# Making all pixel planes of the split maps on ScalarE and GpSimd, with second buffers for them

## The chip, the cores and the metric

The kernel runs on one core of a Trainium2 chip. The core has five engines, each with its own queue that is worked off in order: TensorE (PE in the profile, with PEld for its weight loads), VectorE (DVE), ScalarE (ACT), GpSimd (POOL) and SyncE (SP, which here only issues transfers). They wait for each other by semaphores. The metric is the time of the whole program on the device, in microseconds (us). Three runs of the kernel before took 6669.03, 6680.48 and 6695.74 us, so the median is 6680.48.

## The reference, cut to what matters

The program computes two blocks, one after the other, on four images of 96 channels and 128x128 pixels.

The first block is a state-space layer: projection, depthwise convolution, four directional scans, a layer norm and a projection back to 96 channels. The change does not touch it.

The second block normalises each image and splits it at zero into two maps x1 and x2 (positive and negative part, each with a scale and a shift of its own). From them come three 3x3 convolutions over 96 channels, and a fourth whose weights are made from two of the results:

```python
x, x1, x2 = relu_split_norm(groupnorm(x), ...)
key   = unfold(conv3x3(x1, aw1));  qry = unfold(conv3x3(x2, aw2))
attn  = softmax(key @ qry.T / sqrt(C * 9))            # one set of C x C x 3 x 3 weights per image
out   = conv3x3(conv3x3(x1, aw3), attn)               # and conv3x3(x2, w_conv2) besides
```

A last step normalises the two results, mixes them with a 1x1 convolution and adds the residual.

## The kernel before, in words

**Planes.** For images 1 to 3 the 3x3 convolutions are done with fewer products: along a row, every four output pixels are made from six products, and each product needs one "plane", a fixed combination of neighbouring input pixels. So each map (x1, x2 and the value map v) is kept in DRAM as six planes (`x1p`, `x2p`, `vp`). For input pixels p(k), the six planes are sums and differences of p(k+2) - 4 p(k), of p(k+2) - p(k) and of the latter doubled. `planes_of` (L1354) makes them, for eight rows of 128 pixels and 96 channels at a time (for v: six rows on 128 partitions). It has two ways to do so:

- `at_once` (L1374) does all on VectorE, with nine instructions: L1379, L1380 and L1384 make differences into the tile `diff`, L1386 (two instructions) and L1372 (four) make the planes in the tile `plv`. Every one of them reads both inputs from SBUF.
- `scaled` (L1390) makes two scaled copies on ScalarE, `x4` (L1393, the input times four) and `x2` (L1394, half of it times two). Then `differences` (L1397) makes the planes with ten GpSimd instructions: L1402 to L1407, and four at L1372, into the tile `pl`. L1372 is a helper's line, shared by both ways.

`store_planes` (L1441) sends the finished tile to DRAM from SyncE's queue (L1443).

**The split.** `split_norm` (L1063) goes over an image in 16 tiles of eight rows. For each tile it makes x1 and x2 (L1225 on ScalarE into PSUM, L1229 on VectorE into a tile `half`), and then the planes of each. The argument `vector` chooses the way: in the kernel before, the planes of x1 go by `scaled` and those of x2 by `at_once`. The `half` tiles are two for x1 and one for x2. The scaled copies `x4` have two buffers; `x2`, `pl`, `plv` and `diff` have one.

**The attention.** `attention` (L1925) works on strips of 12 rows. A first pass over 11 strips makes key, query and value (matmuls at L1470 and L1485). ScalarE copies results out of PSUM (L1541), VectorE combines them (L1555 to L1563) into a ring of two strips and into the tile `own`. GpSimd copies 32 channels of each strip from the ring to `own` (L1974, three instructions, twice per strip), and the planes of the value map are made from `own` by `scaled` in two calls per strip (with single buffers). ScalarE also copies shifted inputs (L1904), and transposed pieces for the attention weights (L1751). Then the attention weights are made, and a second pass over 11 strips does the last convolution. Image 0 is done without planes of x1 and x2 (`direct_maps`, with the planes of its value map made by `lift`, L2122, on VectorE); its second pass is the same as that of the others.

**The order of the work.** Each part is a generator that emits instructions and yields a cost. `co_run` (L290) interleaves the attention of image b with a "light" chain: the norm and split of image b+1, and then the closing step of image b-1. `Later` (L305) puts off follow-up steps by some ticks. From the emitted program a scheduler fixes the order of each engine's queue before anything runs. Three splits lie in the program: that of image 1 beside the end of image 0's first pass and its second pass, that of image 2 beside the attention of image 1, and that of image 3 beside the attention of image 2. Image 3's attention runs with no split beside it.

Of the kernel before, what the change touches and what calls it, by code (L numbers as in the profile page):

```python
# [9 lines left out]
F32 = mybir.dt.float32  # L10
# [7 lines left out]
C = 96  # L18
# [15 lines left out]
PB = TN + 1  # L34
PP = PB * TW
# [18 lines left out]
RS = SN // W  # L54
# [14 lines left out]
def kernel(  # L69
# [101 lines left out]
    def col(name, width=1, bufs=None):  # L171
        return small.tile([C, width], F32, name=name, tag=name, bufs=bufs)
# [108 lines left out]
    def part(ps, *shape):  # L281
        n = 1
        for d in shape[1:]:
            n *= d
        t = bank(ps)[: shape[0], :n]
        return t if len(shape) == 2 else t.rearrange("p (a b) -> p a b", b=shape[2])
# [3 lines left out]
    def co_run(left, right, pace):  # L290


        owed = 0.0
        for cost in left:
            owed += cost * pace
            while owed > 0:
                got = next(right, 0)
                if got == 0:
                    return
                if got is None:  # L300
                    owed = 0.0
                    break
                owed -= got
# [39 lines left out]
    def chain(*gens):  # L343
        for g in gens:
            yield from g

    def drain(gen):
        for _ in gen:
            pass
# [713 lines left out]
    def split_norm(xnew, x1d, x2d, stats, keep, cnt, ps, side, planes, vector, done):  # L1063


        with ExitStack() as pools:
# [37 lines left out]
            p2 = p1.enter_context(tc.tile_pool(name="n1", bufs=2, side=side))  # L1104
            for i in range(NS):
                y = ahead.pop(0)
                piece(i + 3)
                r = p2.tile([C, SN], F32, name="xr")
# [12 lines left out]
            p2 = pools.enter_context(tc.tile_pool(name="n2", bufs=2, side=side))  # L1121
# [45 lines left out]
            rs, rh, half = col("rs", 2), col("rh", 2), col("half", 2)  # L1167
# [19 lines left out]
            def stored(i, m, h):  # L1187
# [7 lines left out]
                return lambda: nc.scalar.dma_start(m[:, at : at + RS * PW], h)  # L1195

            half = [
                [p2.tile([C, RS * PP], F32, name=f"half{j}{k}", bufs=1) for k in range(2 - j)]
                for j in range(2)
                if planes  # L1200
            ]
# [2 lines left out]
            for i in range(NS):  # L1204
                y = ahead.pop(0)
                piece(i + 3)
                for side_, m in ((0, x1d), (1, x2d)):
                    op = ALU.is_le if side_ else ALU.is_gt
                    if planes:
                        h = half[side_][i % len(half[side_])]  # L1210
                        v, to = (
                            t.rearrange("p (a b) -> p a b", b=b)[:, :, 0:TN]
                            for t, b in ((y, TN), (h, PB))
                        )
                        k, parts = TW * R, 2
                    else:
# [3 lines left out]
                        v, to = y.rearrange("p (h w) -> p h w", w=W), hv[:, :, 1:PW]  # L1220
                        k, parts = RS, 1
                    for a in range(0, k * parts, k):
                        x, o = v[:, a : a + k], to[:, a : a + k]
                        f = part(ps, C, k, TN) if planes else o
# [24 lines left out]
    def new_planes(name):  # L1249

        m = dram.tile([C, NP, H + 3, TN], F32, name=name, tag=name, bufs=1)
        for h in (0, H + 1, H + 2):
            nc.sync.dma_start(m[:, :, h], zeros[:, 0:TN].unsqueeze(1).to_broadcast([C, NP, TN]))
        return m
# [99 lines left out]
    def planes_of(later, pool, t, r, then, most=RS, vector=False, bufs=2, p=C):  # L1354

        a2 = AA * AA
        v = t[:, : r * PP].rearrange("p (h x) -> p h x", x=PP)

        def planes(name, bufs):
            pl = pool.tile([p, NP, most * TN], F32, name=name, bufs=bufs)[:, :, : r * TN]
            return pl, [pl[:, i].rearrange("p (h t) -> p h t", t=TN) for i in range(NP)]

        def sums(eng, mid, outer, to):
            f1, f2 = mid[:, :, 0:TN], mid[:, :, PB : PB + TN]
            f3, f0 = outer[:, :, 0:TN], outer[:, :, TN:]
            for i, op, x, y in (
                (1, eng.tensor_add, f2, f1), (2, eng.tensor_sub, f2, f1),
                (0, eng.tensor_sub, f2, f0), (5, eng.tensor_sub, f3, f1),  # L1370
            ):
                op(to[i], x, y)  # L1372

        def at_once():  # L1374
            f = pool.tile([p, most, 6 * TN + 4], F32, name="diff", bufs=1)[:, :r]
            mid, outer, df = f[:, :, : 2 * PB], f[:, :, 2 * PB : 130], f[:, :, 130:]
            pl, to = planes("plv", 1)
            stt = nc.vector.scalar_tensor_tensor
            stt(mid, v[:, :, : 2 * PB], -a2, v[:, :, 2 * PB :], ALU.mult, ALU.add)  # L1379
            stt(  # L1380
                outer, v[:, :, 2 * PB : 2 * PB + 2 * TN], -a2, v[:, :, 1 : 1 + 2 * TN],
                ALU.mult, ALU.add,
            )
            nc.vector.tensor_sub(df, v[:, :, 2 * PB :], v[:, :, : 2 * PB])  # L1384
            for i, f in ((3, AA), (4, -AA)):
                stt(to[i], df[:, :, 0:TN], f, df[:, :, PB : PB + TN], ALU.mult, ALU.add)  # L1386
            sums(nc.vector, mid, outer, to)
            later(lambda: then(pl))

        def scaled():  # L1390
            x4 = pool.tile([p, most * PP], F32, name="x4", bufs=bufs)[:, : r * PP]
            x2 = pool.tile([p, most, 2, PB], F32, name="x2", bufs=1)[:, :r]
            nc.scalar.mul(x4, t[:, : r * PP], a2)  # L1393
            nc.scalar.mul(x2, v.rearrange("p h (k b) -> p h k b", b=PB)[:, :, 0:TW:2], AA)  # L1394
            later(lambda: differences(x4.rearrange("p (h x) -> p h x", x=PP), x2))

        def differences(x4, x2):  # L1397
            mid, outer = x4[:, :, : 2 * PB], x4[:, :, 2 * PB : 2 * PB + 2 * TN]
            d1 = x2[:, :, 0, 0:TN]
            pl, to = planes("pl", 1)  # L1400
            sub, add = nc.gpsimd.tensor_sub, nc.gpsimd.tensor_add
            sub(mid, v[:, :, 2 * PB :], mid)  # L1402
            sub(outer, v[:, :, 1 : 1 + 2 * TN], outer)
            sub(to[4], v[:, :, 3 * PB : 3 * PB + TN], v[:, :, PB : PB + TN])
            sub(d1, x2[:, :, 1, 0:TN], d1)
            add(to[3], to[4], d1)
            sub(to[4], to[4], d1)  # L1407
            sums(nc.gpsimd, mid, outer, to)
            later(lambda: then(pl), 2)

        return at_once if vector else scaled
# [829 lines left out]
    class Image:  # L2241
# [27 lines left out]
        def split(self, ps, side, vector=lambda i, second: False):  # L2269
            halves = (self.x1p, self.x2p) if self.b else (self.x1d, self.x2d)  # L2270
            yield from split_norm(
                self.xnew, *halves, self.stats, self.keep, self.cnt, ps, side, self.b > 0, vector,
                self.done,
            )
# [40 lines left out]
    with tc.tile_pool(name="wp", bufs=1, side="left") as wp:  # L2315
# [7 lines left out]
        for images, pace in (([0], 0.25), ([1], 0.75), ([2, 3], 1.35)):  # L2323
            left = projections(images, weights, stats, wp, psl)
            if images[0] == 0:
# [4 lines left out]
                while ready[0] < 2:  # L2330
                    next(left)
                maps = [new_map(n) for n in ("x1d", "x2d", "vd")]
                planes = [
                    [new_planes(f"{n}{i}") for n in ("x1p", "x2p", "vp")] for i in range(2)
                ]
# [9 lines left out]
    imgs = {0: Image(0)}  # L2345
# [9 lines left out]
    psr = ctx.enter_context(tc.tile_pool(name="psr", bufs=2, space=PSUM, side="right"))  # L2355
# [1 line left out]
    imgs[0].lifting = True  # L2357
    light = chain(
        imgs[1].norm(yms[0][1], psr, "right"),
        imgs[1].split(psr, "right", lambda i, second: second),  # L2360
    )
    co_run(left, light, 1.0)
    drain(left)
# [20 lines left out]
    for b in range(NB):  # L2384
        after = []
        if b:
            if b > 1:
                drain(light)
            imgs[b].begin()
            if b + 1 < NB:  # L2390
                imgs[b + 1] = Image(b + 1)
                after.append(imgs[b + 1].norm(yms[(b + 1) // 2][(b + 1) % 2], psr, "right"))
                after.append(imgs[b + 1].split(psr, "right", lambda i, second: second))
            after.append(imgs[b - 1].close(psr, "right"))
        light = chain(light, *after)
        left = imgs[b].attend(at)
        co_run(left, light, 1.0 if b else 1.5)
        drain(left)
# [77 lines left out]
```

## Time and profile before

| | us |
|---|---|
| median of three runs | 6680.48 (6669.03 to 6695.74) |
| the profiled execution | 6664.87 |
| its span in the profile | 6663.1 |
| TensorE busy | 5393.7 |
| VectorE busy | 4885.0 |
| ScalarE busy | 3810.5 |
| GpSimd busy | 3437.4 |

The splits of images 1, 2 and 3 make their planes from 3636 to 4010 us, from 4392 to 4738 us and from 5273 to 5599 us of this span. In each of them VectorE and GpSimd both make 16 sets of planes.

A row for a group of instructions reads: line, engine, operation, output<-input tiles, shapes, x count | busy us, mean ns of one | idle time of the engine just before them, and what ended it. A row for a stretch of time gives the busy us of each engine with the number of its instructions. A row of waits gives who waited for whom, the us in total, how often, and the longest.

### The profile page before, as it was taken

The page shows a single profiled execution, that of the slowest core. Times are in us where ns is not written, and L with a number is a line of the kernel's source. Part 1 is how long each engine was busy: PE and PEld are TensorE (multiplying, and loading weights), DVE is VectorE, ACT ScalarE, POOL GpSimd, SP SyncE. Part 2 cuts the span into 40 slices and gives each one's busy share as a digit, 9 for nine tenths or more (in the row PEclk, how much of TensorE's full clock was granted, in tenths as well). Part 3 has the DMA queues.
Part 4 walks back from the last instruction along what each step waited for, and adds up shares of the span by engine and source line. Part 5 has one row for each costly group of instructions (what it writes and reads, how often), then busy time and mean ns, then how long its engine had stood idle before and what let it go on. Part 6 is the DMA issues. An engine that isn't in the chain of part 4 may idle for free. (4 is left out here: it accounts for less than half of the span.)

```text
span 6663.1 us, 76540 instructions
## 1 busy us (share of the span) xinstructions
PE 5393.7 (81%) x23256; PEld 2343.1 (35%) x23256; DVE 4885.0 (73%) x7737; ACT 3810.5 (57%) x4751; POOL 3437.4 (52%) x2683
## 2 busy tenths in 40 slices
PE   5889978988887626989985579877889777878996
PEld 2333323322221103434433243444333454335642
DVE  3247778988997568979756884588865788887557
ACT  1257768777776576767534554565444664535552
POOL 2236658878786436969622363465124574023410
PEclk9999989988997758999997788988879887989987
DMA  7766777866765666765676766556765555865454
GB/s 166 173 156 180 198 212 199 225 180 171 221 186 162 186 175 208 203 194 175 196 189 175 205 167 165 157 148 163 200 182 159 145 159 153 227 164 145 103 149 143
DMA packets 882102, 1176.27 MB, mean 177 GB/s; under 512 B 215230, under 2 KB 740102, under 8 KB 869212
## 3 DMA queue, kind: packets, MB, share of 16 engines
q1 hardware_dynamic: 858076, 1116.43, 61.9%
q0 software_dynamic: 16208, 38.42, 2.1%
q10 hardware_dynamic: 7408, 16.53, 0.8%
q8 instruction: 187, 3.06, 0.2%
q14 instruction: 223, 1.83, 0.1%
HBM read 766.61 MB, written 334.57 MB: 165 GB/s over the span
## 5 line engine op out<-in xcount | busy, mean ns | idle before, releaser
L621 PE MATMUL bank<-y,wp 128*128 128x512 f32 (+3 forms) x3584 | 1315.3, 623 | 84.3 <-DMA y<-y 34.0
L854 POOL TENSOR_TENSOR y<-y,dl 128x1024 f32<-128x1024 f32 x384 | 1051.3, 2738 | 267.8 <-DVE dl L846 237.1
L821 POOL TENSOR_TENSOR dl<-dl,u 128x1024 f32<-128x1024 f32 x384 | 1007.5, 2624 | 228.0 <-ACT dA L797 116.3
L842 DVE TENSOR_TENSOR_SCAN dA<-dA,pBC 128x512 f32<-128x512 f32 x768 | 981.7, 1278 | 30.7
L1470 PE MATMUL two<-ya,wd 128*64 128x192 f32 (+3 forms) x2376 | 590.5, 426 | 189.5 <-ACT odd L1541 106.6
L735 PE MATMUL pBC<-xr,wbc 60*128 60x512 bf16 (+1 forms) x1536 | 457.1, 402 | 333.8 <-DVE dA L842 260.4
L846 DVE TENSOR_TENSOR dl<-dA,pBC 128x512 f32<-128x512 f32 x768 | 528.8, 689 | 268.2 <-PE pBC L735 195.2
L621 PEld LDWEIGHTS bank<-y,wp 128*128 128x128 f32 (+3 forms) x3584 | 458.3, 169 | 753.5 <-issue 655.5
L2096 PE MATMUL bank<-y,wn 128*128 128x384 f32 (+5 forms) x2408 | 675.2, 503 | 42.2 <-DMA y<-x2d 19.3
L1904 ACT COPY yb<-ya 64x768 f32<-64x768 f32 (+1 forms) x660 | 538.4, 816 | 170.3 <-PE two L1470 121.7
L664 ACT ACTIVATE dl<-pd,dtb 128x512 f32<-128x512 f32 x768 | 486.3, 684 | 185.3 <-PE pd L735 176.9
L1470 PE MATMUL two<-yb,wd 128*64 128x192 f32 (+3 forms) x2376 | 565.2, 410 | 0.0
L825 DVE TENSOR_TENSOR pBC<-dl,pBC 128x512 f32<-128x512 f32 x768 | 527.5, 687 | 9.7 <-POOL dl L821 8.8
L2096 PEld LDWEIGHTS bank<-y,wn 128*128 128x128 f32 (+3 forms) x2408 | 307.4, 167 | 336.8 <-issue 168.7
L1974 POOL COPY own<-ring 32x512 f32<-32x512 f32 (+1 forms) x198 | 219.4, 1144 | 393.7 <-DVE ring L1563 327.0
L797 ACT ACTIVATE dA<-dl,negA 128x1024 f32<-128x1024 f32 x384 | 420.4, 1142 | 2.3
L1470 PEld LDWEIGHTS two<-ya,wd 128*64 128x64 f32 (+1 forms) x2376 | 267.1, 172 | 394.8 <-ACT odd L1541 115.3
L735 PEld LDWEIGHTS <-wbc 60*128 60x128 bf16 (+1 forms) x1536 | 103.5, 96 | 767.9 <-issue 754.2
L664 ACT ACT_TABLE_LOAD x245 | 314.3, 1283 | 99.3 <-PE pd L735 92.0
L1470 PEld LDWEIGHTS two<-yb,wd 128*64 128x64 f32 (+1 forms) x2376 | 293.5, 172 | 151.5 <-issue 43.2
L1470 PE MATMUL two<-ya,wa 128*96 128x384 f32 (+1 forms) x528 | 228.7, 516 | 132.7 <-DMA wa<-watd 86.3
L1001 PE MATMUL bank<-y,outws 96*96 96x512 f32 x512 | 296.7, 710 | 3.5 <-DVE r L1014 2.3
(309 smaller groups left out, 9675.7 us busy)
## 6 DMA issues: line engine op xcount, KB each, us to landing
u<-zb SPq DMA_DIRECT2D x192, 1024.0 KB
yms<-y SPq DMA_DIRECT2D x96, 512.0 KB
y<-yms SPq DMA_DIRECT2D x64, 768.0 KB
xn<-xnew SPq DMA_DIRECT2D x128, 384.0 KB
ya<-vp SPq DMA_DIRECT2D x120, 336.0 KB
y<-y SPq DMA_DIRECT2D x128, 258.2 KB
zb<-z SPq DMA_DIRECT2D x64, 512.0 KB
ya<-x1p SPq DMA_DIRECT2D x90, 336.0 KB
```

Source lines behind the costliest of these rows:

```text
L621: nc.tensor.matmul(blocks(pz[p:e]), lhsT=ws[k][:, d, c : c + e - p], rhs=window(ys[k], at, d, n), start=(i == 0), stop=(i == len(terms) - 1),)
L664: nc.scalar.activation(dst, src, AF.Softplus, bias=bias)
L735: nc.tensor.matmul(p, lhsT=w[rows], rhs=xr[rows, at : at + CH], start=True, stop=True)
L797: nc.scalar.activation(live[m]["dA"], live[m]["dl"], AF.Exp, scale=negA[:, g % 3, k : k + 1])
L821: nc.gpsimd.tensor_mul(t, t, u_view(n))
L825: nc.vector.tensor_mul(p, live[n]["dl"][:, bass.ts(half, CH)], p)
L842: nc.vector.tensor_tensor_scan(h, h, p, init, ALU.mult, ALU.add)
L846: nc.vector.tensor_mul(live[n]["dl"][:, sl], live[n]["dA"][:, sl], live[n]["C", half])
L854: nc.gpsimd.tensor_add(v, v, t.rearrange("p (a b) -> p a b", b=W))
L1470: nc.tensor.matmul(of(to[p:e], r), lhsT=w[:, i, c : c + e - p], rhs=tiles(t[k][PAIR[i]][:, SLOT[i]], o, r), start=(k == 0), stop=False,)
L1904: nc.scalar.copy(yb[k][64 * h - 64 : 64 * h, :, :n], ya[k][0:64, :, h * TN : h * TN + n])
L2096: nc.tensor.matmul(pc[p:e, :n].rearrange("p (h w) -> p h w", w=W), lhsT=w[:, c : c + e - p], rhs=v[:, :, 0:W], start=(i == 0), stop=(i == ...
```

## The change

The planes of x2 are made in the same way as those of x1, so `at_once` and its tiles `diff` and `plv` are no longer used. In their place the `half` of x2, the scaled copy `x2` and the planes `pl` get a second buffer in the split (the value map's calls pass `bufs=1` and keep single buffers).

```diff
@@ split_norm @@
             half = [
-                [p2.tile([C, RS * PP], F32, name=f"half{j}{k}", bufs=1) for k in range(2 - j)]
+                [p2.tile([C, RS * PP], F32, name=f"half{j}{k}", bufs=1) for k in range(2)]
                 for j in range(2)
                 if planes
             ]
@@ planes_of @@
         def scaled():
             x4 = pool.tile([p, most * PP], F32, name="x4", bufs=bufs)[:, : r * PP]
-            x2 = pool.tile([p, most, 2, PB], F32, name="x2", bufs=1)[:, :r]
+            x2 = pool.tile([p, most, 2, PB], F32, name="x2", bufs=bufs)[:, :r]
             nc.scalar.mul(x4, t[:, : r * PP], a2)
@@
         def differences(x4, x2):
             mid, outer = x4[:, :, : 2 * PB], x4[:, :, 2 * PB : 2 * PB + 2 * TN]
             d1 = x2[:, :, 0, 0:TN]
-            pl, to = planes("pl", 1)
+            pl, to = planes("pl", bufs)
@@ the program, twice @@
-        imgs[1].split(psr, "right", lambda i, second: second),
+        imgs[1].split(psr, "right"),
@@
-                after.append(imgs[b + 1].split(psr, "right", lambda i, second: second))
+                after.append(imgs[b + 1].split(psr, "right"))
```

Per partition, the removed tiles held 6,272 bytes (`diff`) and 6,144 bytes (`plv`); the added buffers hold 4,224 (`half`), 2,112 (`x2`) and 6,144 bytes (`pl`).

## The prediction

> **What bounds the kernel now.** I began with the page's totals: TensorE is busy 81% of the span, VectorE 73%, GpSimd 52%. That would make a move from VectorE to GpSimd look free. But the change acts in three stretches only, so I asked for the busy time of each engine in those, beside a stretch with no split. In order: image 0's second pass, image 1's last strips, image 1's second pass, image 2's strips, and image 3's strips with no split.
>
> ```profile
> core 0: us, PE busy (x) PEld busy (x) DVE busy (x) ACT busy (x) POOL busy (x), PEclk, DMA share, GB/s
> 3720.00:3886.00 166.00, 136.38 (x461) 57.18 (x461) 143.78 (x239) 112.78 (x148) 66.77 (x85) 0.93 0.80 218
> 4392.00:4589.00 197.00, 144.06 (x958) 95.95 (x958) 174.83 (x290) 114.24 (x160) 154.47 (x195) 0.83 0.53 140
> 4640.00:4757.00 117.00, 102.26 (x361) 45.83 (x360) 96.79 (x185) 68.22 (x90) 25.06 (x35) 0.93 0.74 204
> 5273.00:5597.00 324.00, 250.51 (x1648) 165.59 (x1648) 281.32 (x477) 185.37 (x255) 249.53 (x313) 0.83 0.52 139
> 6103.00:6347.00 244.00, 231.47 (x1729) 151.16 (x1728) 144.93 (x282) 126.75 (x168) 109.28 (x156) 0.99 0.42 107
> ```
>
> With no split (last row) TensorE is busy 95% of the time, and six strips take 244 us, 40.7 each. Beside a split TensorE falls to 73 and 77%, VectorE stands at 89 and 87%, and GpSimd, far from its mean of 52%, at 78 and 77%. VectorE is nearest to its limit there, but GpSimd has only 43 and 74 us free. The waits between 5273 and 5597 us say how the engines hang together:
>
> ```profile
> PE two L1470 <- ACT odd L1541: 32.9, 6, 9.1
> ACT x L1394 <- POOL pl L1407: 33.8, 14, 7.7
> POOL own L1974 <- DVE ring L1563: 20.2, 4, 7.3
> ```
>
> TensorE waits for ScalarE's copies out of PSUM; ScalarE, whose queue is in order, waits for GpSimd to free the scaled copies, so a late GpSimd can hold back TensorE. GpSimd itself waits for VectorE's evictions into the ring.
>
> The groups of that stretch give the prices (all means in it):
>
> ```profile
> L1372 POOL TENSOR_TENSOR pl<-x 96x256 f32<-96x256 f32 x62 | 47.3, 774 | 0.0
> L1403 POOL TENSOR_TENSOR x<-half,x 96x512 f32<-96x512 f32 x16 | 20.4, 1274 | 0.0
> L1402 POOL TENSOR_TENSOR x<-half,x 96x528 f32<-96x528 f32 x16 | 19.3, 1207 | 15.8 <-ACT x L1393 12.1 <-DVE diff L1384 3.6
> L1404 POOL TENSOR_TENSOR pl<-half 96x256 f32<-96x256 f32 x15 | 9.7, 647 | 10.9 <-DMA x1p<-pl 8.3 <-DVE half L1229 2.1
> L1372 DVE TENSOR_TENSOR plv<-diff 96x256 f32<-96x256 f32 x60 | 44.0, 770 | 0.0
> ```
>
> The two engines need the same time for a 96x256 plane, 774 and 770 ns. That is odd, and it is contention: by the start and end of each record of the plane code, VectorE's L1372 took 412 ns with GpSimd idle beside it and 864 ns with GpSimd busy throughout, while L1229 and L1563, which read one input from PSUM, did not change (737 and 737; 863 and 877 ns).
>
> **What the skill says.** The Trainium skill, SBUF — State Buffer, "Who interferes with whom", says that a VectorE instruction with two SBUF inputs contends with GpSimd instructions that read SBUF, and one with at most one SBUF input does not; the 412, 864 and 737 ns agree. GPSIMD Engine Reference, "3.1 Elementwise — side-by-side cycle accounting", has GpSimd at about twice VectorE's time for a two-input add (4497 against 2293 ns at 2048 elements). GpSimd's 512 elements at L1403 took 1.09 us uncontended, VectorE's at L1380 0.68 us, 1.6 times, so the trace is milder. Perfetto Trace Analysis, "Optimizing Scalar/DVE Operations", warns that moving work between those two might not help because they share a read port; here the sharing goes away with the move, since little else of VectorE's work beside a split has two SBUF inputs.
>
> **The change part by part.** It removes nine VectorE instructions for each of 48 sets. In the trace: L1379 41.4, L1380 47.8, L1384 48.2, L1386 62.0, L1372 118.1, in all 317.5 us, 6.6 us a set; 113.2 of them lie between 5273 and 5597 us. VectorE's share there falls from 87% to (281.3 - 113.2)/324 = 52%.
>
> It adds ten GpSimd instructions a set. The 48 sets of x1 took 413.7 us, 8.6 each, in contention. With VectorE idle beside them the records give 1.10 + 1.09 + 0.64 + 0.73 + 0.68 + 0.68 + 4 x 0.67 = 7.6 us. I take 7.6, since the contending instructions are gone; 8.6 is the other end. It adds 1.07 + 0.65 us of ScalarE a set (L1393, L1394), 27.6 us per image; ScalarE has 139 us free of 324. The number of stores stays; they leave at another time.
>
> The second buffers remove two waits: GpSimd's for the store of the planes before (8.3 us between 5273 and 5597) and ScalarE's for `x2` (part of the 33.8). They do not make GpSimd faster; they let it run without gaps.
>
> What decides is GpSimd's sum where attention strips lie beside the split. Uncontended, the two calls for a strip's value planes cost 0.89 + 0.87 + 0.53 + 0.60 + 0.56 + 0.56 + 4 x 0.56 = 6.3 us each, and an own copy (L1974) 1.09. I counted the work in the changed kernel's GpSimd queue:
>
> - Image 3's split: 32 sets, 12 value calls and 36 own copies up to the end: 32 x 7.6 + 12 x 6.3 + 36 x 1.09 = 243 + 76 + 39 = 358 us. Before, this ran from 5273 to 5597: 324. At 94% occupancy, which leaves it 6% for waits for the ring (20 us before), it needs 381 us: **+56**.
> - Image 2's split: up to the last own copies of the strips, 20 sets, 8 value calls and 21 copies: 152 + 50 + 23 = 225 us against 197; at 94% 239: **+42**. The 12 sets left (91 us) run beside weights and second pass, where GpSimd was nearly idle.
> - Image 1's split: 24 of the sets (182 us) come before the first own copy, for which there were 257 us (3636 to 3893); then 8 sets, 4 value calls and 12 copies, 99 us where there were some 110. **0**.
>
> Gains, where GpSimd has room: the second pass of image 0 has eight x2 sets, 53 us of VectorE's 144 in 166 us. But TensorE is busy 136 and ScalarE comes to 113 + 8 x 1.7 = 127, so I give **-15**; the second pass of image 1, with 97 us of VectorE and 102 of TensorE in 117, **-12**.
>
> The stall of 86.3 us before image 0's second pass (TensorE waits for the weights `wa`, which ScalarE issues after the value planes of image 0) is set by a serial chain: GpSimd clears the tile `lift`, SP loads it, VectorE makes planes, some 3.3 us a round. In the changed queue six sets come before the last six rounds, where three came before the last five. Six sets from 3636 end at about 3692, with the first slowed to some 15 us as before; six rounds and a load then end at 3716 against 3708: **+8**.
>
> Slack: the ring holds two strips, so TensorE may be up to a strip ahead of GpSimd when the first pass ends, and the attention weights need nothing of GpSimd. I credit a third of a strip's 60 us once, **-20**.
>
> Sum: 56 + 42 + 0 - 15 - 12 + 8 - 20 = **+59 us**. The profiled execution of before, 6664.9, becomes 6724; the median is 15.6 above it, so the median becomes **6739**.
>
> **The rivals.**
>
> GpSimd stops ScalarE. With GpSimd without gaps, L1393 and L1394 wait at the head of ScalarE's queue up to a whole set (7.6 us; the longest such wait was 7.7), and behind them stand `odd` and `ends` copies, for which TensorE waits. Occupancy would be 85%: 358/0.85 - 324 = 97 and 225/0.85 - 197 = 68, no gains and no slack, 15 at the lift: +180, **6860**. For it: the waits above; against it: two buffers now stand between the engines.
>
> The gains make up for it. TensorE's slack is a full strip, 60 us, in each of the two splits, so that +56 and +42 vanish nearly, and the second passes gain as said: -15 - 12 + 8 + 20, about 0: **6680**.
>
> VectorE was the bound (the other side). If own copies never hold back the ring, the strips run at the pace that VectorE's relief allows. TensorE's share was 91% between 4000 and 4200 us with no split; at 90% instead of 73 and 77% the two stretches give 33 + 42 us, the second passes 27, less 8 for the lift: -94, **6586**. It decides from the point at which GpSimd's surplus (28 and 34 us at full occupancy) stays below the strip of slack the ring gives. Against it: `own` is a single tile, VectorE may not write the next strip until GpSimd has read the last, and the surplus of the last strips stands before image 3's next load of planes.
>
> **How the numbers follow.** A difference below 0.5%, 33 us, cannot be told from none here. I give the forecast (+20 to +110) 0.45, GpSimd stopping ScalarE 0.2, the balance 0.23, the opposite 0.12. Faster than 6647: 0.12; within 6647 to 6714: 0.23; slower 0.65. The range runs from 6660 (0.12 of the opposite below it, and little else) to 6820 (half of the second case above). The forecast's own range is 6700 to 6790. The price of a set, 8.6 instead of 7.6, would add 32 us to image 3's split and 20 to image 2's; it lies within.
>
> **What would show it.** Right: no VectorE at L1379 to L1386; 96 sets at L1402 on `half` at 7.6 us a set; L1229 and L1563 unchanged; GpSimd busy over 90% for some 380 us in image 3's split, with strips there at about 63 us instead of 57; second passes of images 0 and 1 shorter by 10 to 15 us. Wrong: GpSimd idle more than 10% there with ScalarE waiting for it (then the second case), or strips near 50 us (then the last). It would also be wrong if the lift before image 0's second pass grew by more than 15 us.

## The result and the profile after

The changed kernel took 6760.16 us (median of four runs, 6751.45 to 6765.96), against 6674.75 us for the kernel before in four runs: a ratio of 1.0128, with a 95% interval of 1.0091 to 1.0165. That is slower, as forecast, and by 85 us (61 to 110 by the interval) where 59 were forecast. The profiled execution has a span of 6749.7 us, 86.6 more than that of before, so the two traces can be compared step by step.

The stretches of the changed kernel that answer to those shown of before (image 0's second pass, image 1's last strips, image 1's second pass, image 2's strips, and image 3's strips with no split), as busy us of each engine:

```profile
core 0: us, PE busy (x) PEld busy (x) DVE busy (x) ACT busy (x) POOL busy (x), PEclk, DMA share, GB/s
3737.00:3904.00 167.00, 138.38 (x421) 55.72 (x421) 105.94 (x163) 112.43 (x147) 114.48 (x157) 0.90 0.79 216
4428.00:4650.00 222.00, 150.42 (x958) 97.61 (x958) 106.73 (x204) 128.01 (x178) 196.30 (x278) 0.78 0.45 122
4701.00:4818.00 117.00, 106.69 (x403) 48.98 (x403) 85.22 (x160) 83.10 (x108) 60.65 (x84) 0.97 0.79 221
5326.00:5699.00 373.00, 249.00 (x1683) 164.95 (x1683) 191.74 (x375) 214.97 (x295) 331.76 (x466) 0.81 0.46 126
6194.00:6437.00 243.00, 230.43 (x1737) 150.79 (x1737) 147.39 (x288) 126.68 (x168) 110.37 (x158) 1.00 0.42 108
```

Compare the second and fourth row (image 2's and image 3's strips beside a split) with those of the kernel before: much the same TensorE work (150 and 249 us, before 144 and 251) now lies in 222 and 373 us instead of 197 and 324. VectorE fell from 89 and 87% to 48 and 51%; GpSimd rose from 78 and 77% to 88 and 89%. The last row, with no split, is as it was.

The groups of the changed kernel between 5326 and 5699 us give the price of a set:

```profile
L1372 POOL TENSOR_TENSOR pl<-x 96x256 f32<-96x256 f32 x122 | 82.7, 690 | 0.0
L1402 POOL TENSOR_TENSOR x<-half,x 96x528 f32<-96x528 f32 x32 | 35.5, 1111 | 19.9 <-ACT x L1393 19.7
L1403 POOL TENSOR_TENSOR x<-half,x 96x512 f32<-96x512 f32 x32 | 35.0, 1092 | 0.1
L1404 POOL TENSOR_TENSOR pl<-half 96x256 f32<-96x256 f32 x30 | 19.3, 642 | 3.6 <-DMA x2p<-pl 2.9
```

GpSimd's planes fell from 774 to 690 ns and L1403 from 1274 to 1092 ns. With the other lines of a set (733, 682 and 682 ns) the records of a set add up to 7.7 us. The plane instructions of VectorE are gone (none at L1379 to L1386).

The longest waits in that stretch show whom a late GpSimd stops:

```profile
DVE half L1229 <- POOL pl L1404: 86.1, 17, 14.7
...
PE two L1470 <- ACT odd L1541: 60.6, 8, 12.5
ACT x L1394 <- POOL pl L1407: 55.8, 14, 10.0
ACT x L1393 <- POOL pl L1372: 47.8, 28, 6.0
...
POOL own L1974 <- DVE ring L1563: 14.4, 4, 5.2
```

In the kernel before, between 5273 and 5597 us, two of these were:

```profile
ACT x L1393 <- POOL pl L1372: 22.0, 6, 5.1
DVE half L1229 <- POOL pl L1404: 14.8, 6, 3.4
```

VectorE, relieved of its planes, now stands 86 us in front of a `half` tile that GpSimd has not read yet (15 us before); ScalarE's waits for GpSimd have grown from 56 to 104 us; and TensorE's wait for ScalarE's copies, which stand behind those in the queue, from 33 to 61. GpSimd itself waits less for the ring (14 instead of 20 us).

**Where the 86.6 us came from.** I took eleven landmarks from the start times in both traces. The columns give how much later each is than in the kernel before, and in brackets what was added since the landmark above; "softmax" is the ScalarE instruction of it, "pass" the second pass of an image, "half" the first of that image's split. The other three columns are experiments told below.

| landmark (us in before) | changed | no x2 planes | no x2 planes, two buffers | no x2 planes, two buffers, sums four times |
|---|---|---|---|---|
| softmax of image 0 (3628.7) | 10.8 | 5.4 | 15.7 | 15.2 |
| pass of image 0, first strip (3740.3) | 16.8 (+6.0) | 1.1 (-4.3) | 16.1 (+0.5) | 37.5 (+22.3) |
| its end (3885.1) | 18.2 (+1.4) | 7.3 (+6.2) | 12.8 (-3.3) | 39.6 (+2.1) |
| image 1, fourth strip's copy out (4136.7) | 39.6 (+21.4) | -12.0 (-19.3) | -22.4 (-35.2) | 25.7 (-13.9) |
| half, image 2 (4388.7) | 35.3 (-4.3) | -14.5 (-2.5) | -27.8 (-5.4) | 17.0 (-8.7) |
| softmax of image 1 (4601.2) | 60.5 (+25.2) | -35.9 (-21.4) | -60.5 (-32.7) | 38.8 (+21.8) |
| pass of image 1, end (4777.0) | 56.6 (-3.9) | -50.7 (-14.8) | -77.0 (-16.5) | 32.1 (-6.7) |
| half, image 3 (5269.2) | 53.4 (-3.2) | -48.6 (+2.1) | -82.6 (-5.6) | 32.8 (+0.7) |
| softmax of image 2 (5599.7) | 85.8 (+32.4) | -77.8 (-29.2) | -135.4 (-52.8) | 81.9 (+49.1) |
| pass of image 2, end (5823.1) | 91.3 (+5.5) | -76.1 (+1.7) | -130.5 (+4.9) | 87.4 (+5.5) |
| end (6663.0) | 86.6 (-4.7) | -69.2 (+6.9) | -130.2 (+0.3) | 90.7 (+3.3) |

The first row lies almost wholly before the change takes effect. It was between -7.5 and +24.8 us over all kernels here, so it is mostly the scatter of single executions, and single entries of 10 us mean little. The large ones stand where attention strips run beside a split: +21, +25 and +32. Each column is one execution, so the differences between columns carry that scatter too.

### The profile page after: what moved, and what is told of

Same layout as the page of the kernel before. It is cut to its first block, busy times and chain, and to the rows that moved or that the text cites. A ratio compares the mean times of both kernels' runs of the same rounds, so it can differ in the third digit from the quotient of the medians.

```text
span 6749.7 us, 76711 instructions
## 1 busy us (share of the span) xinstructions
PE 5402.6 (80%) x23256; PEld 2341.8 (35%) x23256; DVE 4626.0 (69%) x7305; ACT 3885.1 (58%) x4847; POOL 3724.4 (55%) x3166
## 5 line engine op out<-in xcount | busy, mean ns | idle before, releaser
L1372 POOL TENSOR_TENSOR pl<-x 96x256 f32<-96x256 f32 (+2 forms) x648 | 410.3, 647 | 0.0
L1555 DVE TENSOR_TENSOR wide<-odd,two 128x192 f32<-128x192 f32 (+5 forms) x176 | 81.7, 464 | 405.9 <-ACT odd L1541 380.1
```

## The experiments

**My theory:** GpSimd's work beside the strips sets the time. **Rivals:** queue order and waits of ScalarE and VectorE for buffers, whatever GpSimd's sum; that VectorE's relief is worth nothing; that all later loss follows from one early shift.

**The move without the second buffers.**

```diff
-                [p2.tile([C, RS * PP], F32, name=f"half{j}{k}", bufs=1) for k in range(2)]
+                [p2.tile([C, RS * PP], F32, name=f"half{j}{k}", bufs=1) for k in range(2 - j)]
-            x2 = pool.tile([p, most, 2, PB], F32, name="x2", bufs=bufs)[:, :r]
+            x2 = pool.tile([p, most, 2, PB], F32, name="x2", bufs=1)[:, :r]
-            pl, to = planes("pl", bufs)
+            pl, to = planes("pl", 1)
```

> The planes of x2 go to ScalarE and GpSimd as in the changed kernel, but the half tile of x2, the scaled copy x2 and the planes pl keep one buffer. GpSimd's sum is what sets the time: the sum stays (358 us of work in image 3's split), but GpSimd now waits some 5 us for the store of the planes before at most of the 96 sets, so its occupancy falls from 94% to some 80%: 30 to 60 us slower than the changed kernel, 6790 to 6820 us. The rival, that queue order and not GpSimd's sum is what costs: within 15 us of the changed kernel, 6745 to 6775 us.

It took 6792.96 us, 1.0181 times the kernel before (1.0151 to 1.0211). So the second buffers give back 33 us of what the move costs. In image 3's split of this kernel the longest waits include:

```profile
ACT x L1394 <- POOL pl L1407: 91.8, 28, 9.4
DVE wide L1555 <- ACT odd L1541: 69.4, 17, 13.0
DVE half L1229 <- POOL pl L1404: 60.3, 11, 12.5
```

ScalarE waits 92 us for the single `x2` tile where it waited 56, and GpSimd's waits for the stores of planes grew from 3 to 20 us. But from `half` to softmax that stretch took 356 us here and 363 in the changed kernel, so these waits did not make it longer. In this trace (of the slowest of the four runs, 27 us above their median) the losses that the changed kernel doesn't have lie elsewhere: image 1's strips lost 35 us (changed kernel: 21), the time between image 1's pass and image 3's split 27 (-3), image 2's second pass, counted from the softmax, 23 (+5). The second of these is image 2's split ending late: its last set was done 8 us after the end of image 1's pass (changed kernel: 23 before it), and the close of image 0 (by the first transfer of its inputs) began 26 us later after that pass than in the kernel before. So the buffers' worth is as large as expected, but not where I expected it, and how it divides among the three buffers stays open.

**Half the move.** In the kernel before:

```diff
-        imgs[1].split(psr, "right", lambda i, second: second),
+        imgs[1].split(psr, "right", lambda i, second: second and i % 2 == 0),
```

(and the same for images 2 and 3)

> The kernel before, with every second x2 set (8 of 16 per image) moved to ScalarE and GpSimd, with the buffers of before. GpSimd's sum sets the time: image 3's split has 24 sets at some 8 us and 115 us of strips' work, 307 us, at 94% 327 us against 324 before, so there is room for half the move: 6660 to 6700 us. The rival, that each moved set costs the same: half of the loss, 6717 us.

It took 6730.77 us, 1.0082 times the kernel before (1.0064 to 1.0101): 56 us more, and both expectations miss. The room I had counted on was not there. The late close after image 1's pass is seen again: of 72.5 us in its trace, 30 lie between that pass and image 3's split, where in the changed kernel nothing was lost. Against the changed kernel this run mixes dose and buffers; the kernel to compare it with is the move without second buffers. There the whole dose cost 119 us, and half of it 56: on equal buffers each moved set costs about the same, as the rival had it.

**No planes of x2.** `then` stores x1's planes into both maps, and the planes of x2 are left out.

```diff
+                    if m is x2d:
+                        return lambda: None
+
                     def then(pl):
-                        store_planes(nc.sync, m, i * RS, RS, pl)
-                        done[m is x2d] = (i + 1) * RS
+                        for to in (x1d, x2d):
+                            store_planes(nc.sync, to, i * RS, RS, pl)
+                        done[0] = done[1] = (i + 1) * RS
```

> Leaves out the planes of x2 altogether (the planes of x1 are stored in their place, so the stores stay): VectorE is relieved as in the change and GpSimd gets nothing. If VectorE was the bound beside the splits: image 2's and 3's strips save some 33 and 42 us, the second passes up to 27, so 6575 to 6610 us. The rival, that the pace of the split or TensorE itself bounds there: within 30 us of before, 6645 to 6705 us.

It took 6598.21 us, 0.9885 times (0.9868 to 0.9902): 76 us less. So the planes of x2 on VectorE did cost time: -19, -21 and -29 us beside the strips by the table. This is not VectorE's relief alone, because GpSimd is relieved too when the contention goes. In image 3's split, before and here:

```profile
5269.00:5600.00 331.00, 252.66 (x1676) 166.86 (x1672) 288.28 (x489) 191.47 (x263) 252.34 (x316) 0.83 0.52 139
5222.00:5522.00 300.00, 237.51 (x1674) 159.41 (x1672) 183.50 (x353) 188.47 (x260) 211.30 (x298) 0.87 0.55 149
```

GpSimd is busy 41 us less (the mean record of its plane code on 96 partitions fell from 862 to 773 ns), and at the price found below, 0.7 us for each, an estimate, that alone could give the 29 us. The two are not separated here. And image 0's second pass got nothing from it (+6.2), although VectorE's load fell there too:

```profile
3741.00:3892.00 151.00, 122.44 (x383) 51.03 (x381) 97.12 (x149) 96.98 (x128) 55.52 (x77) 0.87 0.78 213
```

VectorE is busy 97 of 151 us in that pass, and the pass is no shorter than before (145). VectorE was not its bound.

**The last sums of x2's sets on VectorE.**

```diff
-            sums(nc.gpsimd, mid, outer, to)
+            sums(adder or nc.gpsimd, mid, outer, to)      # adder: nc.vector for x2
```

> The changed kernel, with the last four sums of each x2 set (L1372) on VectorE. GpSimd's sum sets the time: a set of x2 takes 4.9 us of GpSimd instead of 7.6, image 3's split 358 - 43 = 315 us, at 94% 335 against 324, image 2's 198, at 94% 211 against 197, the lift 8, the second passes -10: some 6690 us (6670 to 6715). The rival, that waits at the head of ScalarE's and VectorE's queues cost the time: one more hand-over a set, so no better than the changed kernel, 6750 us or more.

It took 6712.45 us, 1.0055 times (1.0037 to 1.0073), 48 us less than the changed kernel: in the expected range, at its upper end. In image 3's split, though, it gained nothing against the changed kernel. From `half` to softmax, here and in the changed kernel:

```profile
5289.00:5657.00 368.00, 247.01 (x1674) 162.67 (x1674) 233.95 (x415) 212.96 (x291) 299.11 (x406) 0.81 0.46 124
5323.00:5685.00 362.00, 247.12 (x1674) 163.08 (x1674) 183.62 (x355) 212.76 (x291) 321.66 (x452) 0.82 0.46 124
```

GpSimd is busy 299 us instead of 322, and idle 69 instead of 40. A set with its sums on VectorE has one more hand-over between engines, which may be what keeps GpSimd idle; so GpSimd's sum alone doesn't give that stretch, and the expected total came out although the stretch that was to gain most did not gain.

**One image or two.** Image 1's split as in the change and the others as before, and the reverse (each with second buffers where the planes of x2 have moved).

```diff
-        imgs[1].split(psr, "right", lambda i, second: second),
+        imgs[1].split(psr, "right"),
```

> The change for image 1's split alone (second buffers there), images 2 and 3 as before. By the landmarks of the two traces that split cost some 20 to 28 us (lift 6, first strips of image 1 some 21): 6695 to 6705 us. The rival, that GpSimd has room there and the difference is scatter of one execution: within 10 us of before, 6664 to 6685 us.

> The change for images 2 and 3 alone. By the landmarks image 2's strips cost 25, image 3's 32, the second pass of image 1 gives 10 back, image 2's costs 12: 6725 to 6740 us. The rival, that one cause early in the program shifts all that follows: no more than half of the loss, below 6717 us.

They took 6702.42 us, 1.0054 times (1.0034 to 1.0075), and 6734.60 us, 1.0098 times (1.0076 to 1.0120): 37 and 69 us above the kernel before of that call, 6665.64. Both parts cost time, so no single early shift explains the rest. Image 1's part, which I had put at nothing but the lift, is real. The two sum to 106 us where the whole change costs 85; in the trace of image 1's kernel image 3's split took 10 us more, though nothing was changed there. Whether that is the order of the queues or scatter, one trace can't tell, so the 21 us stay unexplained.

**The own copies on ScalarE, and on VectorE.** In the changed kernel:

```diff
-                            nc.gpsimd.tensor_copy(d[:, q:r3:3], v[:, q])
+                            nc.scalar.copy(d[:, q:r3:3], v[:, q])        # or nc.vector.tensor_copy
```

> The changed kernel with the own copies (L1974) on ScalarE. If GpSimd's sum sets the time, image 3's split falls from 358 to 319 us of GpSimd, image 2's from 225 to 202, and the copies no longer stand behind sets: 35 to 60 us faster than the changed kernel, 6700 to 6725 us. The rival, that ScalarE's queue is what is late (it gets 198 copies more): no gain or a loss, 6750 to 6800 us.

> The changed kernel with the own copies (L1974) on VectorE, which the change left half idle. GpSimd's sum falls by 39 us in image 3's split and 23 in image 2's: 35 to 60 us faster than the changed kernel, 6700 to 6725 us, and no slower strips where no split runs. The rival, that the strips wait for VectorE or ScalarE at the head of their queues anyway: within 20 us of the changed kernel, 6740 to 6780 us.

On ScalarE it took 6824.01 us, 1.0237 times (1.0218 to 1.0256), 64 us more than the changed kernel and above both ranges; on VectorE 6741.10 us, 1.0104 times (1.0077 to 1.0130), 19 us less, which is in the rival's range. ScalarE's copies, in the whole of its trace, are as slow as GpSimd's:

```profile
L1974 ACT COPY own<-ring 32x512 f32<-32x512 f32 x180 | 185.7, 1087 | 55.8 <-DVE ring L1563 41.4 <-POOL pl L1404 7.8 <-DVE s L2182 2.5
```

They lengthen the strips with no split from 40.7 to 48.0 us, and image 3's first pass by 58 us. Beside the splits of images 2 and 3 the same kernel lost 15.5 and 20.5 us (changed: 25 and 32), but 14 more in the strips before image 2's split, where the changed kernel won 4; so a gain from GpSimd's relief can't be read off. On VectorE the interval overlaps that of the changed kernel, and 19 us for 62 us of GpSimd's work is a third, less than I had worked out. By the landmarks it was 29 us ahead of the changed kernel at the end of image 2's second pass, and lost 20 of them in image 3's first pass, where no split runs; why, stays open.

**A pure load on GpSimd.** The kernel with no planes of x2, and in each x1 set the last four sums made four times (the sums give the same values each time): 8.0 us more a set by the prices of the prediction, about what an x2 set takes (7.7), with nothing more for ScalarE and VectorE. First with the single buffers of before, then with the second buffers, and there also with no more sums and with the sums made twice.

```diff
-            sums(nc.gpsimd, mid, outer, to)
+            for _ in range(4 if p == C else 1):
+                sums(nc.gpsimd, mid, outer, to)
```

> Leaves out the planes of x2 (those of x1 are stored in their place) and repeats the four last sums of each x1 set three times more on GpSimd: 12 x 0.67 = 8.0 us a set, as much as the x2 set of the changed kernel (7.6), with nothing more for ScalarE or VectorE and no x2 set that holds a half tile or a scaled copy. If GpSimd's sum alone sets the time: back from 6598 to 6740 to 6775 us. The rival, that a good part of the loss comes from ScalarE's and VectorE's waits for buffers held by the added sets: 6640 to 6700 us.

> Leaves out the planes of x2 (those of x1 are stored in their place), with the second buffers of the changed kernel. If second buffers only matter where GpSimd is near its limit: within 15 us of the same with single buffers, 6583 to 6613 us. The rival, that single buffers already hold back the kernel before: 6560 to 6580 us.

> The same with the four last sums of each x1 set made twice on GpSimd, 2.7 us a set. GpSimd's work in image 3's split is then 236 + 43 = 279 us, at 94% 297 against the 300 that this stretch takes without x2 planes: if there is a limit that is reached only then, within 25 us of the kernel with no x2 planes, 6590 to 6625 us. The rival, that every us of GpSimd's work beside the strips is paid in part, limit or not: a third of what three more rounds of sums cost, 6650 us or more.

> The same with the four last sums made four times, 8.0 us more a set, with second buffers. If GpSimd's load alone makes the loss of the changed kernel: 6745 to 6780 us, as the changed kernel (6760), and the 41 us above it of the same dose with single buffers are those of the buffers. The rival, that ScalarE's added copies and the half tiles held by x2 sets make a good part: 6680 to 6730 us.

With single buffers and the sums made four times it took 6801.40 us, 1.0206 times (1.0189 to 1.0223): 203 us more than without, and above what I expected. It compares with the move without second buffers (6793), and with second buffers it should compare with the changed kernel. It does: 6752.24 us, 1.0130 times (1.0101 to 1.0159), against 6760. So GpSimd's load alone gives a loss of the same size; ScalarE's added copies and the x2 sets' hold on `half` tiles are not needed for it. Stretch by stretch the two differ (+49 against +32 in image 3's split, -14 against +21 in image 1's strips), so the match is one of totals. In image 3's split the difference is that of GpSimd's work: it is busy 340 of 380 us here and 322 of 362 in the changed kernel, and idle 40 us in both.

With second buffers and no more sums: 6542.81 us, 0.9815 times (0.9788 to 0.9841). With the sums made twice: 6602.26 us, 0.9903 times (0.9870 to 0.9935). The first missed both its expectations. The second lies in the range stated for "a limit", but only because that range was set around the kernel with single buffers; 59 us above its own base of 6543 it speaks against a limit. The second buffers gained 55 us far from GpSimd's limit (in these kernels each tile of planes is stored twice, which makes a single buffer dearer than in the kernel before). And 2.7 us more a set, 130 us in all, cost these 59 us, where I had expected next to nothing below a limit. The stretch of image 3's split in the three kernels with second buffers, from `half` to softmax, one fence each:

```profile
5187.00:5464.00 277.00, 230.32 (x1674) 155.02 (x1674) 184.41 (x355) 189.77 (x261) 216.98 (x306) 0.90 0.59 162
```

```profile
5225.00:5530.00 305.00, 236.69 (x1682) 157.84 (x1674) 190.67 (x357) 190.37 (x262) 258.15 (x370) 0.87 0.54 147
```

```profile
5302.00:5682.00 380.00, 246.90 (x1674) 162.76 (x1674) 200.46 (x357) 190.79 (x263) 340.16 (x498) 0.78 0.43 119
```

GpSimd is busy 78, 85 and 90%. From the first to the second 41 us of its work cost 28, from the second to the third 82 cost 75. So it is not that there is free room and then a limit: by these three single traces the price of a us on GpSimd is some 0.7 at 80% and 0.9 at 88%, and with a scatter of some 10 us the two prices may be one. The middle kernel's GpSimd is as busy as that of before (258 and 252 us), and its stretch is 26 us shorter (305 and 331); so VectorE's relief and the second buffers together gain something without any relief of GpSimd.

None of the kernels that compute everything was faster than the one before.

## Why the prediction was right, and where it was not

**The cause** was right: GpSimd's work beside the attention strips. With the planes of x2 gone and second buffers there, 128 us are gained (6671 to 6543); GpSimd's load of the same size takes 209 back (6543 to 6752); the sum, 81 us slower than before, is close to the change's 85.

**The total** is near in part by luck. Beside the splits of images 2 and 3 the landmarks give 58 us where 78 were forecast (56 + 42 - 20); image 1's strips cost 21 where nothing was forecast, and image 0's pass gave nothing where 15 were forecast. The first 11 us of the 86.6 are scatter.

**The price of a set**, 7.6 us, was 7.7 by its records. But the records of GpSimd's consecutive instructions overlap a little: in image 3's split 354 us of records are 338 us of busy time, so a sum of prices is some 5% too large. **The removal of contention** was right, as the Trainium skill's page SBUF — State Buffer, "Who interferes with whom", has it: without VectorE's instructions on two SBUF inputs, GpSimd's 774 ns became 690, while VectorE's L1229, with one such input, kept its 0.74 us beside a GpSimd that is busy 89% of the time. (The page says this of instructions outside VectorE's 2-port performance modes, an exception that the prediction left out; the last section has a copy with one SBUF input that does contend.) VectorE at 52% was right too (51%).

**Image 3's split**, +56 by GpSimd's sum at 94%: on GpSimd, from the start of its first set to the end of the last, the stretch grew from 326 to 379 us, +53. Two errors cancel in this: the 358 us of work were 338, and GpSimd was busy 89% of the stretch, not 94. Up to the attention weights it is +32, because the last set now ends 20 us after the softmax has started, where before it ended just ahead of it; this is the slack of 20 that was credited once. **Image 2's split**, +42: up to the last own copy 197 us became 227, +30, and +25 at the landmark. The 225 us of work were 201, at 89% again, so here the term was too large by its work, with hardly any slack.

**The second pass of image 1**, -12: -9.7 between its first and last strip, -3.9 counted from the attention weights. **The lift**, +8: +6.0, within the scatter.

**Image 0's second pass**, -15: this step failed. It took the fall of VectorE's load for a gain, though it named TensorE and ScalarE as near; the pass kept its length, +1.4, and grew no shorter with no planes of x2 at all (+6.2). VectorE did not bound it.

**Image 1's split**, 0: this step failed too. It compared 99 us of GpSimd's work after the first own copy with some 110 us, the time until the last planes were done. By the trace of before that time was 101 us (the last planes of this split were done at 3994 us, not at 4010). But the comparison itself was the wrong one: in the queue nearly all that work stands before the last copies of image 1's second strip, and in the kernel before these were through 89 us after the first own copy had started (3893 to 3982 us). In the changed kernel it took 106 (3920 to 4026), with GpSimd busy 95 of them, and the first copy came 9 us later after the end of image 0's pass. The four strips lost 21 us by the table, and the kernel with image 1's split alone confirms a loss, 37 us in all.

**The second pass of image 2**, which the prediction did not speak of, grew by 12 us from its first strip to its last (+5.5 counted from the attention weights). It did so in the kernels with second buffers and no planes of x2 as well (+11.6 and +11.9), by 6 with single buffers, and not where image 3's split was as before (-3.7). It goes with that split's x2 planes leaving VectorE and not with GpSimd's load; what it is, stays open.

Of the rivals, GpSimd stopping ScalarE at the head of its queue is to be seen in the waits, and VectorE stands there longer still. The sign that the prediction gave for this case, GpSimd idle more than 10% in image 3's split with ScalarE waiting for it, is met, if barely: 11% idle, and 104 us of waits. Its size, +180, is not. The waits are how GpSimd's lateness reaches TensorE and not a loss on top: the pure load made the same time. The opposite case, VectorE as the bound, was half true: to leave out its planes of x2 was worth 76 us, with second buffers 128, in part through GpSimd's own relief, and the load that came with the move cost more. (Its sum was also off: at 90% the two stretches give 37 and 46 us, not 33 and 42.)

## What to carry to other kernels

Before moving work to an engine with a low mean, add up that engine's work in the stretches where the work will run, with uncontended prices, and compare it with their length: here 52% over the span was 77% beside the splits. Don't count room below 100% as free. With in-order queues that wait for each other, a us on GpSimd cost some 0.7 us here at about 80% busy. An experiment that takes work off one engine can relieve another as well, so look at every engine's busy time before you call it that engine's relief. And compare the work with the time until the result that is waited for, not until the last of the work is done: that is where image 1's split was misjudged.

## What was unexpected of the hardware

ScalarE's copy of 32x512 elements from the ring into `own`, which picks every fourth element, took 1087 ns, as long as on GpSimd (1095), while its instruction on 96x512 elements of L1225 took 772 ns in the kernel before. ScalarE's copy also differs in reading and writing SBUF on 32 partitions, so that the step of the reads is the cause is not shown. VectorE did the same copy in 607 ns where GpSimd was idle beside it (120 of 180), and in 1220 ns on average where GpSimd was busy for over 90% of it (44 of them); the longest took 4.0 us, over a row of GpSimd's plane instructions. So this copy, with a single input in SBUF, does contend with GpSimd, while L1229, with one input in SBUF and one in PSUM, does not.
